# End of layer 0 and a turn in `samples`: three edits in a four-layer convolution and attention kernel

## The chip, the cores and the metric

The kernel runs on one core of one Trainium2 chip. The metric is the device time of one execution in microseconds (us). A kernel's time is the median of several executions. The engines run side by side and meet at semaphores: TensorE (PE; its weight loads are PEld), VectorE (DVE), ScalarE (ACT), GpSimd (POOL) and SyncE (SP), which issues loads. Lower is better.

## The reference, cut to what matters

All data are fp32. `x` is 2 x 512 x 32 x 32. Four layers run in sequence; the change touches layer 0 and the MLP that ends it.

```python
# layer 0, cut
xn = _bn(x, bn1_g, bn1_b);  q = _gconv1x1(xn, qw)
off = tanh(einsum(gelu(depthwise_conv(q) + off_dw_b), off_pw_w)) * 4.0      # 8 x 8 sampling points a group
...
kv = _grid_sample(xn.reshape(b * GROUPS, DH, H, W), vgrid_scaled)           # bilinear
k = _gconv1x1(kv, kw);  v = _gconv1x1(kv, vw)
...
pos = grid_q[:, :, None, :] - grid_kv[:, None, :, :]
bias = sign(pos) * log1p(abs(pos))
bias = relu(bias @ cpb_w1 + cpb_b1)                                         # for all 16 groups x 1024 x 64 pairs
bias = relu(bias @ cpb_w2 + cpb_b2)
bias = bias @ cpb_w3 + cpb_b3
attn = softmax(einsum(qh, kh) + bias)
x = x + einsum(attn @ v, out_w) + out_b
h1 = gelu(einsum(_bn(x, bn2_g, bn2_b), mlp_w1) + mlp_b1)
x = x + einsum(h1, mlp_w2) + mlp_b2
# layers 1, 2, 3: group norm and attention with other shapes
```

Most of the time goes into `bias`: a small MLP evaluated for each pair of an image point and a sampling point.

## The kernel before

**Layer 0's main loop.** `layer0` treats eight pairs of groups (`t` = 0 to 7), each with 32 steps `i`, so 256 steps in all. A step takes four sampling points. Each step has four sub-steps `k`, one for each quarter (`part`) of the hidden units. In a sub-step `second` runs 8 matmuls (16 passes, four side by side in column groups) into a two-bank PSUM tile `z`, and ScalarE evicts it with a relu into `h` or another ring (L639). `first` prepares tables for `z` on VectorE (L613), two steps ahead (`AHEAD`). `joined` adds the second of two parts to the first with a sign (L644). A sub-step takes TensorE about 1.72 us.

The two joined halves of a step are then added. One of them is `joins[i - 1]`, the other is `other`, and the adding is done by a DMA with an accumulate, issued by POOL (L970). More such DMAs fold rows of several steps together. For the last four steps (252 to 255) no rows are folded: `third` takes them as they are (its argument `fours`), and step 255's halves are added by VectorE after the loop (L988). `third` (L659) multiplies the sums with the last weights into `sim`, and `scores` (L667) adds the attention scores.

**Work woven in.** The rest of layer 0 (finishing one pair, the offsets of a later one, the sampling of the next) are generators chained into `behind`. On odd `k` the loop advances it by one step, called a turn here: two sub-steps, about 3.44 us, pass from turn to turn. What a generator issues between two `yield`s lands in one turn. `samples(t)` is the one that the change touches. It computes `gpb` (PSUM, L504), then `near` for both axes on ScalarE (L512, L513) with the product of their sums on VectorE (L516), then `wx` and `wy` from `gpb` (L519 to L526), then `pk`, the shift and `kvbd` (L539, L543), `pkv` and `pvo`. `scale_tab` (L601) is not part of it: at every fourth step the loop itself puts a scaling of `tab` ahead of `k` = 0 and one of `pairs` ahead of `k` = 2 on ScalarE.

`z`, `gpb`, `pk`, `pkv`, `pvo`, `pt`, `pa` and `pp` share a PSUM pool of three two-bank buffers (`ps_z`).

**The end of layer 0.** `finish_last` does the last pair: the projection of the first pairs (`project_out`), `third` and `scores` for each half of the 1024 image points, the read of `sim` by ScalarE into `simb` (L743), transposes into `pt` (L753), maxima (L754), the right sums for the MLP (`right_sums`, on POOL and VectorE), 16 exponentials (L761), scaling (L770), transposes of `at` (L775), copies into `aT` (L776), and a closing loop of projections over both halves and four chunks. In that loop `add_out` (L729) adds on VectorE, and `left_sums` forms sums for the MLP's weights.

**The MLP.** `layers` multiplies with Strassen's form in the variant with seven products, so that sums of blocks have to be formed for the weights (`lefts`, L161) and the activations (`rights`, L173 to L176). For the first of eight blocks of pixels, the sums of the second weight matrix (`form2`, kept in `later`) are advanced one by one during the loop over `c`, whatever is left being drained after it. `combined` (L1306 to L1309) turns products into hidden values, `activated` (L1338, L1339) applies gelu. The second product starts at L1374.

**Order.** `in_order` fixes each engine's instructions in the order in which the program issues them. Each engine therefore works through its own list, and an instruction that waits holds everything behind it on that engine.

Of the kernel before, what the change touches and what calls it, by code (L numbers as in the profile page):

```python
# [79 lines left out]
def kernel(ctx: ExitStack, tc: tile.TileContext, a: dict, out: bass.AP):  # L80
# [111 lines left out]
    def layer0(l0, fold_d, t2_b, o2_b):  # L192
# [301 lines left out]
        def samples(t):  # L494
            b, pr = divmod(t, NPAIR)
            xt = one.tile([P, 8, P], F32, name="xt", tag="pixels")
            nc.sync.dma_start(
                out=xt, in_=a["xt"][b, :, pr * P : (pr + 1) * P].rearrange("(k p) c -> p k c", p=P)
            )

            gp = gps.pop(t)
            gpb = zt([P, 2, P], "gpb")
            for ax in range(2):
                nc.tensor.matmul(  # L504
                    gpb[:, ax, :], gp[:, ax : ax + 1].to_broadcast([P, P]), ident, start=True, stop=True
                )
            yield

            near = two.tile([P, 2, 32], F32, name="near")
            wsum = two.tile([P, 3], F32, name="wsum")  # L510
            for ax in range(2):
                nc.scalar.activation(near[:, ax, :], ir, AF.Abs, bias=gp[:, ax : ax + 1], scale=-1.0)  # L512
                nc.scalar.activation(  # L513
                    near[:, ax, :], near[:, ax, :], AF.Relu, bias=1.0, scale=-1.0, accum_out=wsum[:, ax : ax + 1]
                )
            nc.vector.tensor_mul(wsum[:, 2:3], wsum[:, 0:1], wsum[:, 1:2])  # L516
            yield
            wx = one.tile([P, P], F32, name="wx", tag="values")
            nc.scalar.activation(wx, gpb[:, 0, :], AF.Abs, bias=cs("px"))  # L519
            nc.scalar.activation(wx, wx, AF.Relu, bias=1.0, scale=-1.0)  # L520
            wy = one.tile([P, 8, P], F32, name="wy", tag="wy")
            for k in range(8):
                nc.scalar.activation(wy[:, k, :], gpb[:, 1, :], AF.Abs, bias=cs("py", k))
                if k % 3 == 1:
                    yield
            nc.scalar.activation(wy, wy, AF.Relu, bias=1.0, scale=-1.0)  # L526
            yield
            nc.vector.tensor_tensor(wy, wy, wx.unsqueeze(1).to_broadcast([P, 8, P]), ALU.mult)
            yield
            yield  # L530

            pk = zt([P, 2, P], "pk")
            accumulate(pk[:, 0, :], [(xt[:, k, :], wy[:, k, :]) for k in range(8)])
            accumulate(pk[:, 1, :], [(wsum[:, 2:3].to_broadcast([P, P]), ident)])
            ow = one.tile([P, C], F32, name="ow", tag="pixels")
            nc.sync.dma_start(out=ow, in_=a["out_w"][pr * P : (pr + 1) * P, :])
            yield
            shift = one.tile([P, P], F32, name="shift", tag="kq")
            nc.scalar.mul(shift, pk[:, 1, :], col("bn1_b", pr))  # L539
            kv = kvbd[t % 2]  # L540
            for h in range(2):
                r = slice(h * DH, (h + 1) * DH)
                nc.vector.scalar_tensor_tensor(  # L543
                    kv[r, r], pk[r, 0, r], s1[r, pr : pr + 1], shift[r, r], ALU.mult, ALU.add
                )
            yield
            yield
            pkv = zt([P, 2, P], "pkv")
            nc.tensor.matmul(pkv[:, 0, :], kq_w[:, pr, :], kv, start=True, stop=True)
            nc.tensor.matmul(pkv[:, 1, :], bd["vw"][:, pr, :], kv, start=True, stop=True)  # L550
            kq = one.tile([P, P], F32, name="kq", tag="kq")
            nc.scalar.copy(kq, pkv[:, 0, :])
            kqs[t] = two.tile([P, P], F32, name="kqs")
            nc.scalar.mul(kqs[t], pkv[:, 0, :], s1q[:, pr : pr + 1])
            values = one.tile([P, P], F32, name="values", tag="values")
            nc.scalar.copy(values, pkv[:, 1, :])
            yield
            pvo = zt([P, HW], "pvo")
            pb = pvo[:, C : C + 1]
            nc.tensor.matmul(pb, kq, b1q[:, pr : pr + 1], start=True, stop=True)  # L560
            nc.tensor.matmul(pvo[:, :C], values, ow, start=True, stop=True)
            vos[t] = vop.tile([P, C], F32, name="vo")
            nc.scalar.copy(vos[t], pvo[:, :C])
            simbias[t] = two.tile([P, 1], F32, name="simbias")
            nc.vector.tensor_add(simbias[t], pb, col("cpb_b3"))
# [97 lines left out]
        def scores(t, sim, halves=range(2)):  # L663
            b, pr = divmod(t, NPAIR)
            for half in halves:
                n = slice(half * HALF, (half + 1) * HALF)
                nc.tensor.matmul(sim[:, n], kqs[t], xs[b][:, pr, n], start=False, stop=True)  # L667
# [63 lines left out]
        def finish_last(sim, eights, fours, right_sums, left_sums):  # L731

            t, b, pr = NT - 1, B - 1, NPAIR - 1
            halves = [slice(half * HALF, (half + 1) * HALF) for half in range(2)]
            table(AF.Exp)
            pts = [zt([P, 4, P], "pt") for _ in range(2)]
            pps = [zt([P, HW], "pp")]
            project_out(pps[0], b, 0, range(2))
            simb = one.tile([P, HW], F32, name="simb", tag="wy")
            for half, n in enumerate(halves):  # L740
                third(sim, NR - 8, eights, fours, [half])
                scores(t, sim, [half])
                nc.scalar.activation(simb[:, n], sim[:, n], AF.Identity, bias=simbias[t])  # L743
            ptvs = [pt.rearrange("p i (g j) -> p (i g) j", j=NJ) for pt in pts]
            mx = two.tile([P, 16], F32, name="mx")
            at = h2q.tile([P, 8, P], F32, name="at", tag="h2")
            atv = at.rearrange("p i (g j) -> p (i g) j", j=NJ)
            sm = two.tile([P, 16], F32, name="sm")
            for half in range(2):
                g = slice(half * 8, half * 8 + 8)  # L750
                for i in range(4):
                    k = half * 4 + i
                    nc.tensor.transpose(pts[half][:, i, :], simb[:, k * P : (k + 1) * P], ident)  # L753
                nc.vector.tensor_reduce(mx[:, g], ptvs[half], AX.X, ALU.max, negate=True)  # L754
            right_sums()
            pps.append(ps_s.tile([P, HW], F32, name="pp", tag="sim"))
            project_out(pps[0], b, 0, [2])
            project_out(pps[1], b, 1, range(2))
            for half, n in enumerate(halves):
                for g in range(half * 8, half * 8 + 8):  # L760
                    nc.scalar.activation(  # L761
                        atv[:, g, :],
                        ptvs[half][:, g % 8, :],
                        AF.Exp,
                        bias=mx[:, g : g + 1],
                        accum_out=sm[:, g : g + 1],
                    )
                g = slice(half * 8, half * 8 + 8)
                nc.vector.reciprocal(sm[:, g], sm[:, g])
                nc.vector.tensor_tensor(  # L770
                    atv[:, g], atv[:, g], sm[:, g].unsqueeze(2).to_broadcast([P, 8, NJ]), ALU.mult
                )
            for half, n in enumerate(halves):
                for i in range(4):
                    nc.tensor.transpose(pts[half][:, i, :], at[:, half * 4 + i, :], ident)  # L775
                nc.scalar.copy(aTs[b][:, pr, n], pts[half].rearrange("p i j -> p (i j)"))  # L776
                if half == 0:
                    project_out(pps[1], b, 1, [2])
            pps += [zt([P, HW], "pp") for _ in range(2)]
            for half, n in enumerate(halves):  # L780
                for m in range(CC):
                    project_out(pps[m], b, m, range(NPAIR) if m >= 2 else [pr], [half])
                    add_out(b, m, n, pps[m])
                    next(left_sums)
# [143 lines left out]
        for i in range(steps):  # L928
            for k, part in enumerate((1, 0, 3, 2)):
# [37 lines left out]
                        nc.sync.dma_start(out=whole[j:P:4], in_=own[0:P:4])  # L967
                if k == 1 and i - 1 in parts:
                    other = joined(parts.pop(i - 1), 2)
                    nc.gpsimd.dma_start(out=joins[i - 1], in_=other, accum_op=ALU.add)  # L970
                j = (i - 3) % 4
                if k == 1 and 0 <= i - 3 < LAST and j:
                    nc.gpsimd.dma_start(  # L973
# [222 lines left out]
    def layers(f, fold_d, t2_b, o2_b, left1, right1):  # L1196
# [77 lines left out]
        with ExitStack() as mlp:  # L1274
# [57 lines left out]
            for blk in range(NBLK):  # L1332
# [9 lines left out]
                for c in range(MC + 1):  # L1342
# [6 lines left out]
                        upper = combined(pms, p1, hid[:, MC + c, :].rearrange("p (j n) -> p j n", j=2))  # L1349
                    if c:  # L1350
                        form_right2(slice(c - 1, c))
                    if blk == 0 and c >= 4:
                        advance(later[0])
                    if b == 1 and c % 2:
                        advance(norm)
# [952 lines left out]
```

## Time and profile before

| What | Value |
|---|---|
| Median of 3 runs | 3342.02 us (3341.78 to 3342.47) |
| The profiled execution | 3342.55 us |
| Its span, first to last instruction | 3340.7 us |
| Mean granted TensorE clock | 0.999 |
| Layer 0's main loop, by TensorE's first and last `z` matmul | about 53.6 to 1964.7 us |
| End of layer 0 (`finish_last`) | about 1964.7 to 2006.8 us |
| MLP's second product of the first block begins | 2031.9 us |

A line of a timeline has the start, the duration, the engine, the line of the code, the operation, what is written and read, and how many instructions were merged; in brackets the engine's idle time before it and what ended it. A line of the waits has the waiting instruction, what it waited for, and the total us, the times and the longest. Two stretches of `finish_last`, to show how much of each engine is free there:

```profile
1979.40:1988.60 9.20, 8.86 (x33) 4.66 (x32) 4.60 (x10) 6.15 (x34) 0.35 (x1) 1.00 0.01 2
1988.60:2006.80 18.20, 17.35 (x42) 7.43 (x40) 15.66 (x37) 0.59 (x1) 0.20 (x1) 1.00 0.00 0
```

The columns are the stretch, its length, the busy time of PE, PEld, DVE, ACT and POOL, the granted clock (1 is full), and the DMA engines' share and GB/s.

### The profile page before, as it was taken

The page shows a single profiled execution, that of the slowest core. Times are in us where ns is not written, and L with a number is a line of the kernel's source. Part 1 is how long each engine was busy: PE and PEld are TensorE (multiplying, and loading weights), DVE is VectorE, ACT ScalarE, POOL GpSimd, SP SyncE. Part 2 cuts the span into 40 slices and gives each one's busy share as a digit, 9 for nine tenths or more (in the row PEclk, how much of TensorE's full clock was granted, in tenths as well). Part 3 has the DMA queues.
Part 4 walks back from the last instruction along what each step waited for, and adds up shares of the span by engine and source line. Part 5 has one row for each costly group of instructions (what it writes and reads, how often), then busy time and mean ns, then how long its engine had stood idle before and what let it go on. Part 6 is the DMA issues. An engine that isn't in the chain of part 4 may idle for free.

```text
span 3340.7 us, 60894 instructions
## 1 busy us (share of the span) xinstructions
PE 3316.0 (99%) x24789; PEld 1600.6 (48%) x24789; DVE 2642.5 (79%) x3033; ACT 1812.4 (54%) x2763; POOL 675.3 (20%) x806
## 2 busy tenths in 40 slices
PE   9999999999999999999999999999999999999999
PEld 4333333333333333333333339999953443687777
DVE  7999999999998899999999966455446465665556
ACT  4866877877876677877867642112136245122221
POOL 1333333333333233333333210000000000000000
PEclk9999999999999999999999999999999999999999
DMA  5887787787777587787787741000100000000111
GB/s 178 165 167 150 158 167 159 156 168 154 161 161 157 109 168 152 163 163 158 162 165 155 154 119 58 14 11 11 52 0 14 26 33 16 7 7 4 29 33 36
DMA packets 142993, 343.92 MB, mean 103 GB/s; under 512 B 36976, under 2 KB 51952, under 8 KB 141936
## 3 DMA queue, kind: packets, MB, share of 16 engines
q0 software_dynamic: 68400, 231.26, 37.1%
q1 hardware_dynamic: 71056, 102.12, 10.2%
q10 hardware_dynamic: 3248, 6.56, 0.5%
q8 instruction: 197, 3.23, 0.4%
q14 instruction: 92, 0.75, 0.1%
HBM read 71.46 MB, written 10.83 MB: 25 GB/s over the span
## 4 chain that ended last, share of the span: by engine, by line
PE 96%; DVE 1%; issue 1%; ACT 1%; DMA 0%; ACTq 0%; POOL 0%; DVEq 0%; POOLq 0%
PE z L630 52%; PE pma L135 6%; PE pw L1471 6%; PE pmb L135 5%; PE pmv L1471 4%; PE score L1650 3%; PE pv L1662 3%; PE pm L1471 3%; PE score L1471 3%; PE pmt L1471 1%; PE ppr L1471 1%; PE sim L659 1%; PE pf L135 1%; PE pp L719 1%; PE pma L1374 1%
## 5 line engine op out<-in xcount | busy, mean ns | idle before, releaser
L630 PE MATMUL z<-wa,cpb_w 128*32 128x512 f32 x10880 | 1192.2, 593 | 3.4 <-ACT h L639 3.4
L639 ACT ACTIVATE h<-z,b2h 128x1024 f32<-128x1024 f32 x768 | 852.1, 1115 | 329.2 <-PE z L630 300.4
L613 DVE CUSTOM_DVE_ANT_1 wa<-tab,pairs 128x2048 f32<-128x2048 f32 x340 | 779.9, 2295 | 2.9 <-PE z L630 2.5
L630 PEld LDWEIGHTS z<-wa,cpb_w 128*32 128x32 f32 x10880 | 346.2, 110 | 809.7 <-issue 713.6
L630 PE MATMUL z<-h,cpb_w 128*32 128x512 f32 x5504 | 609.4, 593 | 0.7 <-ACT h L639 0.7
L613 DVE CUSTOM_DVE_ANT_1 h<-tab,pairs 128x2048 f32<-128x2048 f32 x172 | 394.7, 2295 | 1.3 <-PE z L630 1.0
L630 PEld LDWEIGHTS z<-h,cpb_w 128*32 128x32 f32 x5504 | 175.6, 110 | 407.9 <-issue 364.3
L644 DVE SCALAR_TENSOR_TENSOR h<-h,turn,h 128x1024 f32<-128x1024 f32 x256 | 329.8, 1288 | 5.5 <-ACT h L639 5.5
L639 ACT ACTIVATE bridge<-z,b2h 128x1024 f32<-128x1024 f32 x162 | 181.1, 1118 | 118.6 <-PE z L630 118.6
L963 POOL DMA_DIRECT2D bridge<-bridge x150 | 127.6, 850 | 530.6 <-DMA bridge<-h 498.1
L644 DVE SCALAR_TENSOR_TENSOR bridge<-bridge,turn,h 128x1024 f32<-128x1024 f32 x162 | 208.3, 1286 | 5.2 <-ACT bridge L639 5.2
L970 POOL DMA_DIRECT2D bridge<-h x161 | 151.7, 942 | 289.3 <-DVE h L644 175.1
L1314 ACT COPY p<-pma 128x128 f32<-128x128 f32 x80 | 21.4, 267 | 334.4 <-PE pma L135 313.3
L1306 DVE TENSOR_TENSOR upper<-pma,p 128x256 f32<-128x256 f32 x80 | 33.8, 422 | 178.5 <-ACT p L1314 178.4
L1651 ACT ACTIVATE p<-score 128x512 f32<-128x512 f32 x256 | 130.3, 628 | 81.0 <-PE score L1650 79.9
L963 POOL DMA_DIRECT2D h2j<-h2j x90 | 76.2, 847 | 313.0 <-DMA h2j<-h 304.2
L639 ACT ACTIVATE h2j<-z,b2h 128x1024 f32<-128x1024 f32 x94 | 105.1, 1118 | 41.8 <-PE z L630 41.2
L1683 DVE TENSOR_TENSOR acc<-acc,p 128x1024 f32<-128x1024 f32 x96 | 111.2, 1219 | 19.8 <-ACT p L1651 19.5
L1650 PE MATMUL score<-q,k 64*128 64x512 f32 x512 | 120.7, 604 | 1.1 <-DVE gm L1227 1.1
L644 DVE SCALAR_TENSOR_TENSOR h2j<-h2j,turn,h 128x1024 f32<-128x1024 f32 x94 | 121.3, 1290 | 0.0
L1662 PE MATMUL pv<-p,vT 128*64 128x512 f32 x512 | 116.5, 598 | 0.0
L973 POOL DMA_DIRECT2D bridge<-bridge x90 | 108.4, 1204 | 3.2 <-DMA bridge<-bridge 2.5
(463 smaller groups left out, 4369.5 us busy)
## 6 DMA issues: line engine op xcount, KB each, us to landing
bridge<-h POOLq DMA_DIRECT2D x161, 512.0 KB, 5.2
h2j<-h POOLq DMA_DIRECT2D x94, 512.0 KB, 5.5
bridge<-bridge POOLq DMA_DIRECT2D x159, 256.0 KB, 3.6
tab<-slog_d SPq DMA_DIRECT2D x128, 256.0 KB, 5.0
h2j<-h2j POOLq DMA_DIRECT2D x90, 256.0 KB, 3.2
bridge<-bridge POOLq DMA_DIRECT2D x150, 128.0 KB, 5.2
bridge<-bridge SPq DMA_DIRECT2D x90, 128.0 KB, 3.9
bridge<-h2j SPq DMA_DIRECT2D x90, 128.0 KB, 3.7
```

Source lines behind the costliest of these rows:

```text
L135: nc.tensor.matmul(pm, w, m, start=(k == 0), stop=(k == len(pairs) - 1))
L613: nc.vector._custom_dve(TENSOR_ADD_SAT, out=h1, in0=tx.unsqueeze(1).to_broadcast([P, H, 2, W]), in1=ty.unsqueeze(3).to_broadcast([P, H, 2, ...
L630: nc.tensor.matmul(z[point * 32 : point * 32 + 32, n], cpb_w2[:, lo : lo + 32], h1s[point][:, half * 16 : half * 16 + 16, :], start=True, ...
L639: nc.scalar.activation(h2, z, AF.Relu, bias=b2h[:, part : part + 1])
L644: nc.vector.scalar_tensor_tensor(h2, h2, turn[:, part // 2 : part // 2 + 1], parts.pop(part + 1), ALU.mult, ALU.add)
L963: nc.gpsimd.dma_start(out=own[0:P:2], in_=own[1:P:2], accum_op=ALU.add)
L970: nc.gpsimd.dma_start(out=joins[i - 1], in_=other, accum_op=ALU.add)
L1471: nc.tensor.matmul(out, stationary(l, k), moving(r, k), start=start and k == 0, stop=k == nk - 1, skip_group_check=not start,)
L1650: nc.tensor.matmul(sc, ks[m][r, s * P : (s + 1) * P], qs[m][r, n], start=True, stop=True)
L1651: nc.scalar.activation(p[:, part], sc, AF.Exp, scale=64 ** -0.5)
L1662: nc.tensor.matmul(pv[half][part * 64 : part * 64 + 64], vt[s % 4][:, lo : lo + 64], lps[s, half][:, part, :], start=(s == 0), stop=(s == 7),)
L1683: nc.vector.tensor_add(acc[half], acc[half], ps[s, half])
```

## The change

Four edits, in the order of the program:

1. In `samples`, a `yield` between the two axes of `near`: the second axis is issued one turn later, and everything after it in `samples` too.
2. In `finish_last`, `third` and `scores` of both halves are issued before either half of `sim` is read by ScalarE. `project_out` of chunk 0, pair 2 moves up between the scores and the reads; on TensorE it stood behind the transposes.
3. In the main loop, the sums of steps 253 and 254 are made by VectorE (`tensor_add`) in place of POOL's adding DMA.
4. In the MLP's loop over `c`, the sums of the second weight matrix are advanced at `c` = 4, 5, 6 and no longer at 7 and 8; what is left is drained after the loop, as before. At 8 there was nothing left to issue, so one sum moves: the fourth of the first chunk.

```diff
@@ samples @@
                     near[:, ax, :], near[:, ax, :], AF.Relu, bias=1.0, scale=-1.0, accum_out=wsum[:, ax : ax + 1]
                 )
+                if ax == 0:
+                    yield
             nc.vector.tensor_mul(wsum[:, 2:3], wsum[:, 0:1], wsum[:, 1:2])
             yield
@@ finish_last @@
-            for half, n in enumerate(halves):
+            for half in range(2):
                 third(sim, NR - 8, eights, fours, [half])
                 scores(t, sim, [half])
+            project_out(pps[0], b, 0, [2])
+            for n in halves:
                 nc.scalar.activation(simb[:, n], sim[:, n], AF.Identity, bias=simbias[t])
...
             right_sums()
             pps.append(ps_s.tile([P, HW], F32, name="pp", tag="sim"))
-            project_out(pps[0], b, 0, [2])
             project_out(pps[1], b, 1, range(2))
@@ the main loop of layer0 @@
                 if k == 1 and i - 1 in parts:
                     other = joined(parts.pop(i - 1), 2)
-                    nc.gpsimd.dma_start(out=joins[i - 1], in_=other, accum_op=ALU.add)
+                    if i < steps - 2:
+                        nc.gpsimd.dma_start(out=joins[i - 1], in_=other, accum_op=ALU.add)
+                    else:
+                        nc.vector.tensor_add(joins[i - 1], joins[i - 1], other)
@@ layers @@
-                    if blk == 0 and c >= 4:
+                    if blk == 0 and 4 <= c < MC - 1:
                         advance(later[0])
```

`steps` is 256 and `MC` is 8.

## The prediction

> **What bounds the kernel now.** I read the busy shares first, then TensorE's waits, then the timelines around each wait.
>
> ```profile
> PE 3316.0 (99%) x24789; PEld 1600.6 (48%) x24789; DVE 2642.5 (79%) x3033; ACT 1812.4 (54%) x2763; POOL 675.3 (20%) x806
> ```
> ```profile
> PE z L630 <- ACT h L639: 4.1, 6, 0.7
> ...
> PE sim L659 <- DMA bridge<-h: 2.1, 1, 2.1
> ...
> PE pma L1374 <- ACT hid L1339: 0.9, 1, 0.9
> ...
> PE sim L659 <- ACT simb L743: 0.8, 1, 0.8
> ...
> PE pt L753 <- ACT simb L743: 0.3, 1, 0.3
> ```
>
> TensorE is idle for only 3340.7 - 3316.0 = 24.7 us. No matmul is removed, so all the change can win is idle time and any slow clock behind it. The columns are total us, times, longest. Six equal waits of 0.68 us lie in layer 0's main loop. Those on `sim` and `pt` lie at its end.
>
> ScalarE's timeline at one of the six (start, duration), then TensorE's:
>
> ```profile
> 442.84 1.12 ACT L639 ACTIVATE bridge<-z,b2h 128x1024 f32<-128x1024 f32 x1 [0.60 <-PE z L630]
> 443.85 0.31 ACT L512 ACTIVATE near<-ir,gp 128x32 f32<-128x32 f32 x1
> ...
> 445.00 0.82 ACT L601 ACTIVATE pairs<-tab,pc 128x512 f32<-128x512 f32 x1
> 445.73 2.10 ACT L639 ACTIVATE h<-z,b2h 128x1024 f32<-128x1024 f32 x2
> ```
> ```profile
> 446.87 3.64 PE L630 MATMUL z<-h,cpb_w 128*32 128x512 f32 x32 [0.67 <-ACT h L639]
> ```
>
> Two evictions of `z` have 445.73 - 443.85 = 1.88 us of other work between them: `near` of both axes (1.15) and `pairs` (0.73). TensorE stands 0.67 us, so 1.88 - 0.67 = 1.21 us would fit.
>
> The end of layer 0, on TensorE:
>
> ```profile
> 1968.37 1.06 PE L659 MATMUL sim<-bridge,w 128*32 128x512 f32 x6
> 1971.51 0.62 PE L659 MATMUL sim<-bridge,w 128*32 128x512 f32 x1 [2.09 <-DMA bridge<-h]
> ...
> 1973.77 2.07 PE L667 MATMUL sim<-x,kqs 128*128 128x512 f32 x2
> 1976.62 1.06 PE L659 MATMUL sim<-bridge,w 128*32 128x512 f32 x8 [0.78 <-ACT simb L743]
> ...
> 1978.47 1.13 PE L667 MATMUL sim<-x,kqs 128*128 128x512 f32 x2
> 1979.44 0.60 PE L753 MATMUL pt<-cst,simb 128*128 128x128 f32 x4
> 1980.38 0.66 PE L753 MATMUL pt<-cst,simb 128*128 128x128 f32 x4 [0.34 <-ACT simb L743]
> ```
>
> The chain of waits names the transfer of the 2.09 us, and the stage table (PE, PEld, DVE, ACT, POOL busy; granted clock; DMA) what follows it:
>
> ```profile
> 1960.99 10.48 DMA bridge<-h
> ```
> ```profile
> 1973.00:1975.00 2.00, 2.00 (x3) 0.50 (x2) 0.00 (x0) 0.00 (x0) 1.05 (x2) 0.50 0.00 0
> ```
>
> It is step 254's adding DMA (L970). The same view over narrower stretches gives 0.87 for 1972.5 to 1973.0 and 0.72 for 1976.0 to 1976.5: half clock from about 1972.86 to 1976.27.
>
> **What the Trainium skill says.** "TensorE: Matmul & The Clock Gate", Part 1: after an idle window of about 3.4 us, counted by a free-running clock, TensorE runs at half rate until it was busy for one. The trace agrees: half clock for about 3.41 us behind a 2.09 us wait. "VectorE: DVE Perf Modes", the section on the TRN2 errata: an fp32 tensor_tensor add takes (N + 151)/0.96 ns, 1224 for N = 1024; L988, such an add, took 1.23 us. "DMA: Bandwidth & Descriptors", Anatomy of one DMA: about 2.0 us plus bytes/436e3, 3.2 us for 512 KB. Here the measurement decides: the page's median is 5.2 us, and this one took 10.48 while the 4 MB of `mlp_w1` (issued at 1958.00) moved.
>
> **The change part by part.**
>
> *Last steps summed by VectorE.* Two L970 DMAs (steps 253 and 254) go, with POOL's issue; two 1.23 us adds come. `joined` for them runs at 1952.29 and 1959.16 (1.28 each), and VectorE then idles 2.15 us before its next (1955.73, 1962.60). The adds fit there and end at about 1954.8 and 1961.7. What is late next is step 255's sum, unchanged at 1967.34 + 1.23 = 1968.57. `third` starts at 1968.37 and needs it in its second round, 0.86 us later: no wait.
>
> *Both halves scored first.* With all sums there, a half costs what the second does now: 1976.62 to 1978.47 for `third` (1.85), then about 0.9 for the scores. So 1968.37 + 2 x 2.75 = 1973.87. `project_out` of pair 2 follows: 4 passes of 0.43 = 1.72, to 1975.59. Behind it ScalarE reads. I assume that the first read waits for the last score (end 1972.97 + 1.13 = 1974.10), since today the second half's matmuls wait for a read of the first. Two reads of 0.69 end by about 1975.4, before TensorE wants them, so the 0.78 and 0.34 go. Queued behind the first read on ScalarE, which now waits longer, are only the second read and the exponentials. POOL's next, the `normed_rights` (L185), waits for `third` as today and is done by about 1975, before VectorE wants it.
>
> But these 1.72 us lay behind the transposes and covered the softmax; that cover is gone. From the first transpose (1979.44 today), by VectorE's timeline (ends of L770), the first half's weights are ready at 1984.31, 4.87 later, and the second half's (bound by 16 exponentials at 0.29) at 1986.70, 7.26 later; the second half's transposes needn't wait now, but the exponentials follow the first maximum just as soon. New: transposes at 1975.59 and 1976.02, then 8 passes to 1979.89; weights at 1980.46: idle 0.6. Transposes 0.43 and 4 passes 1.72 to 1982.6; second weights at 1982.85: idle 0.25. Its transposes end, and the closing loop begins, at 1983.3; today at 1988.62.
>
> Gain: 5.3 us. As a sum: 2.28 of stall start to start, 0.86 (the late sum sent TensorE through its column groups once more), 1.5 of half clock over the 2.98 busy us from 1972.86, 0.94 and 0.51 for the two reads with pipeline drain, minus 0.85 of new idle: 5.2. The closing loop (17.2 us of matmuls, VectorE 2.1 us per chunk in step) shifts whole. Bounds: if the softmax chain runs 1 us longer, 4.3; if nothing stands, 6.1.
>
> *A turn between the axes.* The turn with `pairs` now holds 0.57 + 0.73 = 1.30 us against 1.21 that fit: a wait of about 0.1 instead of 0.68, so 6 x 0.57 = 3.4 won. The second axis (0.57 alone) hides in the next turn. Everything after it in `samples` comes 3.44 us later: VectorE's `wsum` (0.15), the matmuls of `pk`, `pkv` and `pvo`, and SP's load of `ow`, which still has four turns until `pvo` reads it. So `gpb` holds its PSUM slot a turn longer, and collisions must be read again. In the six: `wx` with two `wy` (1.16), three `wy` twice (0.75), `relu` (0.94) all fit; `pk` now meets `pairs`, with 2.2 us of TensorE's own work beside it. In the fifth sample (t = 4, near at 1195.34), the first three `wy` now meet `tab`, 0.75 + 0.71 = 1.46 with the slot still held: about 0.25 lost. In the eighth they meet when the slot is being freed, as t = 4 does now without a wait. VectorE is nearly full here (first 2.2 and joined 1.2 in a turn of 3.44), but its tables are finished at least 3.4 us before TensorE reads them (starts of L613 against L630, all 256 steps), and recover; 0.6 us fewer per sample leaves that. Net 3.1; bounds 2.0 and 4.1 (no wait left).
>
> *MLP's last sum behind.* The fourth left sum of chunk 0 (1.22 us at 2036.32) moves behind the last right sums:
>
> ```profile
> 2032.60 1.42 DVE L161 TENSOR_TENSOR wb<-wb 128x1024 f32<-128x1024 f32 x1
> ...
> 2036.32 1.22 DVE L161 TENSOR_TENSOR w2s<-wb,w2s 128x1024 f32<-128x1024 f32 x1
> ```
>
> The 0.91 us wait at L1374 comes from the sum at 2032.60, ahead of the last `combined`, and that stays. The right sums come 1.2 us earlier, but TensorE wants them only at 2038.61, 0.5 us after they are ready today. The moved sum feeds product 3, at 2045.76. If that cover were gone, the right sums' 1.2 us would be what is won or lost. I take 0; the bounds are no gain (the sums end at the same 2043.1) and 0.9 (the wait gone after all).
>
> Sum: 5.3 + 3.1 + 0 = 8.4 us. The profiled execution took 3342.55 (span 3340.7 and 1.85 around it): 3334.15 expected. The median lies 0.53 lower: 3342.02 - 8.4 = 3333.6.
>
> **Rivals.**
> A, likeliest (0.66): as above, 3333.6; its own range 3332.0 to 3335.2 (gains 10.0 and 6.8).
> B (0.16): the end gains 5.3, the turn nothing: with `gpb` held longer, new collisions give back what `near` gave. For it: the slack is only 1.21, and 1.16 and 1.30 lie beside it. Against it: equal contents stand in t = 4 and t = 7 without a wait. 3336.7.
> C (0.12): the turn gains 3.1, but the end becomes bound by the softmax chain: new idle of about 2.5 instead of 0.85, perhaps with half clock again (1.5). For it: the exponentials alone are 4.7 us in a row. Against it: the distances above are measured. 5.3 - 1.7 - 1.5 = 2.1 left of the end; 3342.0 - 5.2 = 3336.8.
> D, slower (0.06): VectorE's queue. By its timeline it stood 1.13 us at `kvbd` (L543, 474.93) for ScalarE's `shift`, with the next table and `joined` queued behind it. If the later place makes that hold long enough to use up the 3.4 us lead, each further us is TensorE's. From about 4.5 us a sample it starts to cost; at 6, 8 x 1.5 = 12 lost against 8.4 won, 3345.6. Against it: the lead there is 5 to 6 us, and `shift` now stands alone in its turn.
>
> **How the numbers follow.** A measurement here tells about 0.2% from no change, 6.7 us: faster means below 3335.3. A lies nearly all there (0.66, of it 0.62). B and C lie within 0.2% but for their quicker tails (0.28, of it 0.10 faster). Of D, 0.05 is slower and 0.01 within. So faster 0.62 + 0.10 = 0.72, same 0.04 + 0.18 + 0.01 = 0.23, slower 0.05. The range for 8 in 10 is 3331.6 to 3337.4: A whole, and most of B and C.
>
> **What would show it.** Right: TensorE's waits without `DMA bridge<-h` and without `simb`; no half clock between 1965 and 1990; idle of 0.6 and 0.25 at the `at` transposes (L775 now); the six waits at about 0.1, and one of 0.25 near 1205. Wrong: a new wait of over 1 us at these transposes, waits of `z` elsewhere in `samples`, or a shift in L1374's wait.

## The result and the profile after

| | before | after |
|---|---|---|
| median of the runs, us | 3341.53 (3339.19 to 3344.57, 16 runs) | 3334.59 (3334.02 to 3335.76, 16 runs) |
| span of the profiled execution, us | 3340.7 | 3332.7 |

The ratio is 0.998, with a 95% interval from 0.9973 to 0.9987: the kernel became faster by 6.9 us, 0.21% of its time. The forecast was 3333.6. The profiled pair differs by 8.0 us in its spans. Its parts are these, each read as a distance in us between the starts of two groups of matmuls on TensorE (the marks of before, then those of after, in brackets):

| stretch | before | after | gain |
|---|---|---|---|
| first `z` matmul of layer 0's main loop to the start of `third` (53.61 to 1968.37; 53.66 to 1966.16) | 1914.76 | 1912.50 | 2.3 |
| start of `third` to the start of the closing loop (1968.37 to 1988.62; 1966.16 to 1981.46) | 20.25 | 15.30 | 4.95 |
| closing loop to the MLP's second product (1988.62 to 2031.93; 1981.46 to 2024.77) | 43.31 | 43.31 | 0 |
| a stretch of the values stage of a later layer (2853.72 to 2857.91; 2846.44 to 2850.00) | 4.19 | 3.56 | 0.6 |
| all the rest | | | 0.2 |

First the busy shares of the kernel after, to set against the line of before:

```profile
PE 3314.5 (99%) x24789; PEld 1599.7 (48%) x24789; DVE 2645.3 (79%) x3035; ACT 1813.7 (54%) x2763; POOL 673.7 (20%) x804
```

The counts show the edit: two instructions more on VectorE, two fewer on POOL, the same matmuls. TensorE's idle time fell from 24.7 us to 3332.7 - 3314.5 = 18.2 us, and its busy time by 1.5 us. That is as much as the half clock cost in before, and it didn't come here. TensorE's waits in the kernel after:

```profile
PE pma L1380 <- ACT hid L1345: 0.9, 1, 0.9
...
PE pt L778 <- DVE at L773: 0.5, 1, 0.5
...
PE z L632 <- ACT h L641: 0.2, 1, 0.2
```

The three waits at the end of layer 0 (on the transfer of `bridge`, and twice on `simb`) are gone; one of 0.5 at the transposes of `at` is new. Of the six waits on `z` only one small wait is left in the list. The MLP's 0.9 stayed. The edits add lines, so L630 of before is L632 here, L775 is L778, and L1374 is L1380. Now TensorE at the end of layer 0:

```profile
1966.16 1.07 PE L661 MATMUL sim<-bridge,w 128*32 128x512 f32 x8
...
1968.01 1.13 PE L669 MATMUL sim<-x,kqs 128*128 128x512 f32 x2
1969.07 1.06 PE L661 MATMUL sim<-bridge,w 128*32 128x512 f32 x8
...
1970.92 1.12 PE L669 MATMUL sim<-x,kqs 128*128 128x512 f32 x2
1971.89 1.88 PE L721 MATMUL pp<-aT,vo 128*128 128x512 f32 x4
1973.60 1.04 PE L757 MATMUL pt<-cst,simb 128*128 128x128 f32 x8
1974.48 3.60 PE L721 MATMUL pp<-aT,vo 128*128 128x512 f32 x8
1978.62 0.63 PE L778 MATMUL pt<-cst,at 128*128 128x128 f32 x4 [0.55 <-DVE at L773]
1979.08 1.88 PE L721 MATMUL pp<-aT,vo 128*128 128x512 f32 x4
1980.99 0.63 PE L778 MATMUL pt<-cst,at 128*128 128x128 f32 x4
1981.46 17.33 PE L721 MATMUL pp<-aT,vo 128*128 128x512 f32 x40
```

`third` and its scores now run twice in a row without a stop, `project_out` of pair 2 at 1971.89 covers the reads of `sim`, and the one new stop is the 0.55 at 1978.62. Last, ScalarE at the place where before it held TensorE up for 0.67 us (start, duration):

```profile
442.46 1.12 ACT L641 ACTIVATE bridge<-z,b2h 128x1024 f32<-128x1024 f32 x1 [0.60 <-PE z L632]
443.47 0.31 ACT L512 ACTIVATE near<-ir,gp 128x32 f32<-128x32 f32 x1
...
444.05 0.82 ACT L603 ACTIVATE pairs<-tab,pc 128x512 f32<-128x512 f32 x1
444.78 2.26 ACT L641 ACTIVATE h<-z,b2h 128x1024 f32<-128x1024 f32 x2
446.93 0.31 ACT L512 ACTIVATE near<-ir,gp 128x32 f32<-128x32 f32 x1
...
450.65 0.36 ACT L521 ACTIVATE wx<-gpb,cst 128x128 f32<-128x128 f32 x1
```

The second axis of `near` (444.43 in before) moved to 446.93, and `wx` follows a turn later. What lies between two evictions of `z` is now 444.78 - 443.47 = 1.31 us in place of 1.88.

### The profile page after: what moved, and what is told of

It is laid out like the page before. It is cut to its first block, busy times and chain, and to the rows that moved or that the text cites. A ratio compares the mean times of both kernels' runs of the same rounds, so it can differ in the third digit from the quotient of the medians.

```text
span 3332.7 us, 60901 instructions
## 1 busy us (share of the span) xinstructions
PE 3314.5 (99%) x24789; PEld 1599.7 (48%) x24789; DVE 2645.3 (79%) x3035; ACT 1813.7 (54%) x2763; POOL 673.7 (20%) x804
## 4 chain that ended last, share of the span: by engine, by line
PE 97%; DVE 1%; issue 1%; ACT 1%; POOL 0%; ACTq 0%; DVEq 0%; POOLq 0%
PE z L632 52%; PE pma L135 6%; PE pw L1477 6%; PE pmb L135 5%; PE pmv L1477 4%; PE score L1656 3%; PE pv L1668 3%; PE pm L1477 3%; PE score L1477 3%; PE pmt L1477 1%; PE ppr L1477 1%; PE pp L721 1%; PE sim L661 1%; PE pf L135 1%; PE pma L1380 1%
## 5 line engine op out<-in xcount | busy, mean ns | idle before, releaser
L632 PE MATMUL z<-wa,cpb_w 128*32 128x512 f32 x10880 | 1193.1, 593 | 0.5
L632 PEld LDWEIGHTS z<-wa,cpb_w 128*32 128x32 f32 x10880 | 345.9, 110 | 806.3 <-issue 714.1
L632 PE MATMUL z<-h,cpb_w 128*32 128x512 f32 x5504 | 609.4, 593 | 0.3 <-ACT h L641 0.2
L632 PEld LDWEIGHTS z<-h,cpb_w 128*32 128x32 f32 x5504 | 175.4, 110 | 409.6 <-issue 360.6
```

The source lines that it names most:

```text
L632: nc.tensor.matmul(z[point * 32 : point * 32 + 32, n], cpb_w2[:, lo : lo + 32], h1s[point][:, half * 16 : half * 16 + 16, :], start=True, ...
```

## The experiments

The theory was the sum of the prediction; the rivals were that the turn gives nothing (B), that the softmax chain takes the end's gain back (C), and later some on what is left. Distances in a trace are given as "start of `third` to closing loop" and "first `z` to start of `third`", because the start of layer 0 itself shifts by up to 2 us from one execution to the next.

### The adds alone (e1_adds)

The kernel before, with edit 3 only.

```diff
-                    nc.gpsimd.dma_start(out=joins[i - 1], in_=other, accum_op=ALU.add)
+                    if i < steps - 2:
+                        nc.gpsimd.dma_start(out=joins[i - 1], in_=other, accum_op=ALU.add)
+                    else:
+                        nc.vector.tensor_add(joins[i - 1], joins[i - 1], other)
```

> Before, with only the sums of steps 253 and 254 moved to VectorE. My theory: the 2.09 us wait for the DMA goes, and with it the second pass through the column groups (0.86) and the half clock behind it (1.5): third's start to the closing loop falls from 20.25 to about 15.6 us, the two waits on simb (0.78, 0.34) stay, total -4.6 us. Rival (the order does it, the sums were as good as hidden): under 1 us.

Measured: 3337.51 against 3341.83 (ratio 0.9988, 0.9982 to 0.9995), so 4.3 us; in the trace `third` to closing loop takes 1984.63 - 1968.88 = 15.75, 4.5 less than before. No half clock came there. TensorE's timeline of this kernel still shows the two reads:

```profile
1972.64 1.06 PE L659 MATMUL sim<-bridge,w 128*32 128x512 f32 x8 [0.78 <-ACT simb L743]
...
1976.39 0.65 PE L753 MATMUL pt<-cst,simb 128*128 128x128 f32 x4 [0.34 <-ACT simb L743]
```

So two adds of 1.23 us on an engine that idled there bring nearly the whole gain of the end. Both sums were moved at once; that step 254's was the one that counted is read from the wait in before, and no run moved it alone.

### The order alone (e2_order), and both (e3_both)

The kernel before with edit 2 only, and with edits 2 and 3.

```diff
-            for half, n in enumerate(halves):
+            for half in range(2):
                 third(sim, NR - 8, eights, fours, [half])
                 scores(t, sim, [half])
+            project_out(pps[0], b, 0, [2])
+            for n in halves:
...
-            project_out(pps[0], b, 0, [2])
```

> Before, with only both halves scored ahead of the reads and project_out of pair 2 moved up. My theory: the wait for the DMA and the half clock stay, the waits on simb go (1.45 with drain) and 0.5 to 1.1 us of new idle at the transposes of at comes: -0.4 us, within -1.2 to +0.5. Rival (the order does it): -4 us or more.

> Before, with the two edits of the end together. My theory: -5.0 us, as the trace of after shows for third's start to the closing loop (15.30), so little more than the adds alone give; no half clock. Rival (the two multiply, as one alone leaves the other's wait): far more than the sum of the single ones.

Measured: the order alone 3341.03 (0.9999, 0.999 to 1.0007), not told from before; both together 3337.21 (0.9986, 0.998 to 0.9993), 4.6 us faster. In the traces, `third` to closing loop takes 18.52 and 15.27. With the adds there (15.75 to 15.27), the order brings 0.5 us; the medians differ by 0.3, which is too little to be told by itself. Alone it keeps the wait for the transfer and adds its own new one, as TensorE's timeline of the order alone shows:

```profile
1972.05 0.62 PE L659 MATMUL sim<-bridge,w 128*32 128x512 f32 x1 [2.21 <-DMA bridge<-h]
...
1984.48 0.63 PE L776 MATMUL pt<-cst,at 128*128 128x128 f32 x4 [0.53 <-DVE at L771]
```

That execution had a surprise: no half clock followed the 2.21 us. So of the 20.25 - 18.52 = 1.73 us that it takes less than before, about 1.5 are the half clock that didn't come, and only some 0.2 are the order. In its table of stretches (PE, PEld, DVE, ACT, POOL busy; granted clock; DMA) the stretch around the stall reads:

```profile
1970.00:1975.00 5.00, 2.95 (x12) 0.72 (x16) 0.00 (x0) 0.00 (x0) 0.93 (x2) 1.00 0.69 262
```

### The turn alone (e4_turn)

The kernel before with edit 1 only.

```diff
+                if ax == 0:
+                    yield
```

> Before, with only the yield between the axes of near. My theory from the trace of after: six gaps of 1.29 us become 0.72 (-3.4), 0.14 comes back at each of the turns of wx (8 times, -0.3 of it at t = 4 and 7 offset by near itself), and 0.36 at t = 4 where wy meets tab: -2.2 us at the start of third. As predicted first: -3.1. Rival (the turn moves the waits elsewhere): 0.

Measured: 3339.05 against 3341.83 (0.9991, 0.9983 to 1.0), 2.8 us by the medians; in the trace the start of `third` comes 2.4 us earlier after the first `z`. The stall of 2.2 us and the half clock stay. B falls, and the size is 2.4, not 3.1.

### The kernel after again (e5_after), and before again (e12_before)

The first is the kernel after, beside the next three on the same chip; the second is the kernel before, executed once for its trace.

> The changed kernel once more, as the base for the three edits beside it: 3334.6 us median; in its trace no half clock at the end of layer 0, the six gaps of z at 0.72 us.

> Before once more, for its trace alone. If the half clock behind the 2.1 us wait hangs on where the wait falls in a free-running window, it may be missing or shorter this time, as it was in the run with the order alone (2.21 us wait, full clock); third's start to the closing loop is then 18.7 instead of 20.25 us. If a 2 us wait always brings it: 20.25 again.

Measured: 3335.07 for after (0.9978, 0.9971 to 0.9986) against 3341.71. In its trace there is no half clock at the end of layer 0, the six gaps are 0.71 to 0.72 us, and `third` to closing loop takes 15.27. The one execution of before took 3341.11. Its profile has the stall (2.00 us) and the half clock, and `third` to closing loop takes 20.44, but the half clock began at another place relative to the stall; the same stretch of its table:

```profile
1970.00:1975.00 5.00, 3.61 (x7) 0.84 (x8) 0.00 (x0) 0.00 (x0) 0.16 (x1) 0.67 0.60 230
```

The stretch of the values stage is also 0.7 us shorter (3.46) than in the first profile of before.

### The new idle time at the end (e6_split)

The kernel after, with one half of pair 2's `project_out` kept behind the transposes, to cover the softmax.

```diff
-            project_out(pps[0], b, 0, [2])
+            project_out(pps[0], b, 0, [2], [0])
...
             pps.append(ps_s.tile([P, HW], F32, name="pp", tag="sim"))
+            project_out(pps[0], b, 0, [2], [1])
```

> After, with half 0 of project_out of pair 2 left ahead of the transposes and half 1 put behind them again. If the new idle at the transposes of at (0.55 and 0.2 us) is the cover that the move took from the softmax, it goes: third's start to the closing loop 14.5 instead of 15.30 us, -0.8 us. Rival (the softmax chain itself is late for another reason, the reads of simb for one): no gain, or the idle turns up ahead of the transposes.

Measured: 3334.51 against 3335.07 for after. `third` to closing loop takes 14.62, 0.68 less than the kernel after; the medians differ by 0.6, which is too little to be told by themselves. TensorE's timeline:

```profile
1979.86 0.60 PE L779 MATMUL pt<-cst,at 128*128 128x128 f32 x4
...
1982.01 0.60 PE L779 MATMUL pt<-cst,at 128*128 128x128 f32 x4
```

Neither group of transposes waits: the 0.55 was the cover that pair 2 took with it when it moved.

### What is left of the six waits (e7_scale), and without the turn (e10_noturn)

The kernel after, with `pairs` and `tab` (`scale_tab`) issued behind the eviction of `second` in place of ahead of it; then the same without the `yield`.

```diff
             for k, part in enumerate((1, 0, 3, 2)):
-                if i % 4 == 1 and k % 2 == 0 and i // 4 + 1 in tabs_of:
-                    scale_tab(i // 4 + 1, k // 2)
...
                 parts.setdefault(i, {})[part] = second(i, four, part)
+                if i % 4 == 1 and k % 2 == 0 and i // 4 + 1 in tabs_of:
+                    scale_tab(i // 4 + 1, k // 2)
```

> After, with the scalings of tab and pairs issued behind the sub-step's second instead of ahead of it, so that an eviction lies between them and the turn's work. If the remaining gaps come from these two standing in one space between evictions, the six gaps fall from 0.72 to 0.43 and the loss of 0.36 at t = 4 goes: -2.0 us. If ScalarE's sum over the sub-steps decides, not the single space: 0 to -0.5.

> The kernel with the scalings behind the eviction, but near of both axes in one turn as before (no yield). If what counts is the work between two evictions (about 1.2 us fit), near's 1.15 alone fits nearly, and the yield was one way of two to get near and pairs apart: within 0.5 us of the run with the yield (3331.9). If the yield is needed by itself: +2 us.

Measured: 3331.87 with the turn (0.9971, 0.9959 to 0.9983), 3.2 us below e5_after, more than expected; in the trace the time from the first `z` to `third` is 2.9 us shorter than in after (2.7 than in e5_after): about 0.29 at each of the six, 0.08 at one more place in each of `t` = 1 to 7, and 0.38 at `t` = 4. Without the turn 3334.35 (0.998, 0.9972 to 0.9988), and `third` starts 2.6 us later than with it. The expectation that the turn would then be worth at most 0.5 failed, and its rival (+2) came. Against e3_both, which has neither, the moved scalings alone give 2.4 us in the trace, as much as the turn alone gave in e4_turn. So the two are not two ways to the same gain: they add. ScalarE's timeline with the turn, then without:

```profile
444.93 0.31 ACT L512 ACTIVATE near<-ir,gp 128x32 f32<-128x32 f32 x1
...
445.64 1.11 ACT L641 ACTIVATE h<-z,b2h 128x1024 f32<-128x1024 f32 x1
446.65 0.83 ACT L603 ACTIVATE pairs<-tab,pc 128x512 f32<-128x512 f32 x1
447.38 1.11 ACT L641 ACTIVATE h<-z,b2h 128x1024 f32<-128x1024 f32 x1
```

```profile
443.48 0.31 ACT L512 ACTIVATE near<-ir,gp 128x32 f32<-128x32 f32 x1
...
444.61 1.10 ACT L639 ACTIVATE h<-z,b2h 128x1024 f32<-128x1024 f32 x1
445.61 0.83 ACT L601 ACTIVATE pairs<-tab,pc 128x512 f32<-128x512 f32 x1
446.34 1.10 ACT L639 ACTIVATE h<-z,b2h 128x1024 f32<-128x1024 f32 x1
447.34 0.37 ACT L519 ACTIVATE wx<-gpb,cst 128x128 f32<-128x128 f32 x1
...
448.45 1.11 ACT L639 ACTIVATE h<-z,b2h 128x1024 f32<-128x1024 f32 x1
```

In the second, three spaces in a row (a space is what lies between two evictions) are full, with 1.13, 0.73 and 1.11 us. No single one is as full as before's 1.88, yet the six waits are there again, at 0.2 each:

```profile
PE z L630 <- ACT h L639: 1.2, 6, 0.2
```

Lateness that one eviction doesn't catch up is carried to the next. In the first kernel `wx` comes a turn later, behind an idle space of ScalarE.

### The MLP's wait (e8_mlp), and its sum (e11_mlp_sum)

First the kernel after with the sums of the second matrix advanced at `c` = 3, 4, 5, so that none lies ahead of the last `combined`; then the kernel before with edit 4 only.

```diff
-                    if blk == 0 and 4 <= c < MC - 1:
+                    if blk == 0 and 3 <= c < MC - 2:
```

> After, with the weight sums advanced at c = 3, 4, 5 instead of 4, 5, 6. If the 0.91 us wait at the second product comes from the sum ahead of the last combined (as predicted, and why the fourth edit moves nothing), it goes: -0.9 us. Rival (it is ScalarE's gelu): it stays.

> Before, with only the fourth edit (the fourth weight sum behind the last right sums): 0 us, the 0.91 us wait at the second product unchanged. Rival (VectorE's order there sets the product's start): -0.9.

Measured: 3334.48 for the first, 0.6 below e5_after by the medians, too little to be told by themselves, and 0.80 in the trace from the product's first matmul to the group behind it (4.90 in after, 4.10 here). TensorE's timeline of the kernel after, then of this one:

```profile
2024.77 3.43 PE L1380 MATMUL pma<-hid,wb 128*128 128x128 f32 x28
2029.12 0.71 PE L1380 MATMUL pma<-hid,wb 128*128 128x128 f32 x4 [0.92 <-ACT hid L1345]
2029.67 1.95 PE L135 MATMUL pma<-hid,wb 128*128 128x128 f32 x16
```

```profile
2024.74 4.26 PE L1380 MATMUL pma<-hid,wb 128*128 128x128 f32 x32
2028.84 1.95 PE L135 MATMUL pma<-hid,wb 128*128 128x128 f32 x16
```

The wait is gone, so it was the sum ahead of the last `combined`, and not the one that edit 4 moves. Edit 4 alone gives 3341.77 against 3341.26 (1.0, 0.9992 to 1.0008), with the 0.9 unchanged.

### The three that helped, together (e9_all)

The kernel after with the edits of e6_split, e7_scale and e8_mlp.

> After, with the three edits that each gained: half of the projection behind the transposes, the scalings behind the eviction, the weight sums one step earlier. They lie in three stages that follow each other, so the gains should add: -0.7 - 2.8 - 0.8 = -4.3 us in the trace, about 3330.6 us; half of that if one is hidden by another.

Measured: 3330.54 (0.9966 of before, 0.9952 to 0.998), span 3328.7, against 3334.59 for after. Against the trace of after the gains add: 2.84 to the start of `third`, 0.68 at the end, 0.80 in the MLP.

## Why the prediction came true, and where its sizes were off

The forecast was faster by 8.4; the medians give 6.9 and the spans of the profiled pair 8.0. Case A holds. The time itself missed by only 1.0 us (3333.6 against 3334.59), and half a microsecond of that nearness is luck: the median of before over 16 runs lies 0.5 below the one over 3 runs from which the forecast started. The single edits add up to about the whole: 4.6 (e3_both) and 2.8 (e4_turn) by the medians, against 6.9 and, in e5_after, 6.6. The steps:

**The end, 5.3 predicted.** 4.95 in the profiled pair, and 4.6 by the medians of e3_both. The step was right in its parts, and the runs split its sum in two: stall, second pass through the column groups and half clock are 2.28 + 0.86 + 1.5 = 4.6, and the adds alone measured 4.5 in the trace; the two reads less the new idle are 1.45 - 0.85 = 0.6, and the order on top of the adds measured 0.5. The assumption that ScalarE's first read waits for the last score held: in the kernel after it begins at 1972.09, behind the scores that start at 1970.92. Two sizes were off: from the first transposes to the weights it takes 1978.62 - 1973.60 = 5.02 us, not 4.87, and a pair of scores 1.0 from start to start (0.97 and 1.06), not 0.9. The first stop at the transposes was 0.55 (0.6 predicted) and the second 0.2 from start to start (0.25 predicted), so rival C's 2.5 didn't come. e6_split shows that this new idle time was the lost cover, as the prediction had it.

One term, the 1.5 us of half clock, isn't in every execution. Of the five profiles with a stall of 2.0 to 2.2 us here (before, e2_order, e4_turn, e11_mlp_sum, e12_before) four have it and e2_order doesn't (the last section shows what parts them). The prediction says that the trace agrees with "TensorE: Matmul & The Clock Gate" of the Trainium skill (Part 1); that is so for the length of the half clock (3.41 us), and not for the idle time ahead of it, which was 2.09 and not 3.4. That the half clock is missing in some executions may also be why before's runs spread over 5.4 us and after's over 1.7. The runs' mean clocks point the same way: in the three sets of runs of before that list them (57, 35 and 26 runs), the 23 at 1.000 have medians 1.8, 1.6 and 1.5 us below those at 0.999; for after it is 0.2 (6 and 9 runs, e5_after). Without their traces this is not shown.

**The turn, 3.1 predicted.** 2.3 in the profiled pair and 2.4 in e4_turn. The 0.57 at each of the six places was exact: the distance between the starts of the two `z` passes there fell from 1.29 to 0.72 us (0.43 where nothing waits). What was mis-sized is the room, "1.88 - 0.67 = 1.21 us would fit". The 0.67 is the idle column of TensorE; start to start, TensorE lost 1.29 - 0.43 = 0.86 there, 0.19 more than that column shows. So 1.88 - 0.86 = 1.02 us fit. With this room, worked out after the runs, the places that the prediction costed at nothing or too low come out within 0.1 us of what was measured:

| between two evictions of `z` | us | less 1.02 | measured |
|---|---|---|---|
| one axis of `near`, `pairs` | 1.31 | 0.29 | 0.29 (regained in e7_scale) |
| `wx`, two `wy`, eight times | 1.11 | 0.09 | 0.11 to 0.14 lost |
| three `wy`, `tab`, at `t` = 4 | 1.46 | 0.44 | 0.36 lost |
| both axes of `near`, at `t` = 4 and 7 in before | 1.15 | 0.13 | 0.13 to 0.17 won |

The sum is 6 x 0.57 + 2 x 0.15 - 8 x 0.12 - 0.36 = 2.4. In before the `wx` group came directly behind the stall and cost nothing; that it was the stall which made room for it is my reading, and no run shows it by itself. The single room isn't the whole rule either, as e10_noturn showed: in a row of full spaces the evictions' own 1.01 us leave 3.44 / 2 - 1.01 = 0.71 us a space on the long run, and 1.02, so 0.31 more, only for one that comes after an idle one. By this estimate the three spaces of e10_noturn lose 1.13 + 0.73 + 1.11 - 3 x 0.71 - 0.31 = 0.53 us; 0.46 was measured at each of the six places.

**The MLP's sum, 0 predicted.** e11_mlp_sum shows no change, and e8_mlp that the wait belongs to the sum that stayed, as the prediction said.

**Rivals.** B fell with e4_turn, C with e1_adds and e3_both. D: in the kernel after, no wait of TensorE on `z` is for a table of VectorE's; the only one in the list is for ScalarE's `h`.

**The rest of the 8.0.** 0.6 us came in the stretch of the values stage, which the change doesn't touch: VectorE waited 2.05 us for the transfer `r<-d` in before, and 1.42 in after. It isn't the change's: the unchanged kernel in e12_before had it too (1.31), and the kernel after lost most of it again in e5_after (1.88). This is part of why the profiled pair shows more than the medians do.

## What to carry to other kernels

A wait's idle column can be less than what the wait costs (0.67 against 0.86 here); take the distance from start to start of the matmuls around it against the undisturbed distance, and size the room for moved work by that. When several small groups of work share an engine with a periodic duty, add up successive spaces and not only one, since lateness is carried over. A sum that ends a chain of transfers, moved to an engine that idles there, can be worth more than the reordering around it: here 4.5 of the 5 us.

## What was not expected of the hardware

**Whether half clock follows a stall of 2 us hangs on where the stall lies in a fixed grid of time.** In each of the five traces the changes of the clock that it records lie whole multiples of 3.413 us apart, from the start of the program to its end. From the end of the half clock behind the stall to the half clock at the end of the program, for one, it is 1361.92 us in all four (399 steps). So the grid can be laid over the stall, in e2_order too, where the half clock at the end of the program begins at 3335.46 and a step therefore ends at 3335.46 - 1361.92 = 1973.54. The steps around the stall and those behind it, in before and then in e2_order (columns as in the tables of stretches above; the figure behind the first comma is TensorE's busy time, and the third from the end is the clock):

```profile
1969.45:1972.87 3.42, 1.36 (x6) 0.36 (x6) 0.00 (x0) 0.00 (x0) 0.00 (x0) 1.00 1.02 376
1972.87:1976.28 3.41, 2.97 (x4) 0.50 (x2) 0.00 (x0) 0.40 (x1) 1.09 (x2) 0.50 0.03 12
```
```profile
1966.72:1970.13 3.41, 3.12 (x11) 0.74 (x10) 2.23 (x2) 0.00 (x0) 0.00 (x0) 1.00 1.04 310
1970.13:1973.54 3.41, 1.49 (x6) 0.36 (x6) 0.00 (x0) 0.00 (x0) 0.00 (x0) 1.00 0.98 374
1973.54:1976.96 3.42, 3.42 (x16) 0.85 (x16) 0.00 (x0) 0.00 (x0) 1.08 (x2) 1.00 0.01 2
```

In before all but 0.03 us of the stall lies in one step, which is idle for 3.42 - 1.36 = 2.06 us, and the next step is at half clock from end to end. In e4_turn, e11_mlp_sum and e12_before the stall lies within one step too, with 2.20, 2.23 and 1.99 us of idle time, and the next is at half clock. In e2_order a border of the grid cuts the stall into 0.29 and 1.92 us, and the clock stays full. So in these five traces the line lies between 1.92 and 1.99 us of idle time in one step, with a single case on its near side. It isn't the whole rule: e3_both, e6_split, e7_scale and e11_mlp_sum have a step at half clock near the start of the program (15.1 to 18.7) behind one with only 0.79 us of idle time. "TensorE: Matmul & The Clock Gate" (Part 1) of the Trainium skill says that the window is free-running, which agrees with the grid; but by the page it takes an idle window of about 3.4 us, and here about 2 us within one were enough.

**A transfer under load.** The adding transfer of 512 KB took 10.48 us in before while the `mlp_w1` load moved; the median of its kind is 5.2. The DMA engines' share is 1.02 in that stretch (1960.99 to 1971.50) and 0.68 in the 7.1 us before it. That the load made it so long is read from this; no run moved the load. In its place VectorE's add took 1.23.

**The start of the program.** The first `z` begins up to 2 us later in some profiled executions, whatever the kernel: e3_both, e6_split, e7_scale and e11_mlp_sum have a mean clock of 0.66 between 15 and 20 us and begin `z` 1.8 to 2.0 us later, before and after don't. Differences of a profiled pair below 2 us should be read from marks inside the stage, not from the spans.
